# Cross attention in fp32 by three-part products: turned values through a DRAM tile, and an order planned from both ends

## The chip, the cores and the metric

The kernel runs on one core of one Trainium2 chip. The metric is device time in microseconds (us) of one execution of the whole program. TensorE (PE) multiplies, with its weight loads shown apart as PEld; VectorE (DVE), ScalarE (ACT) and GpSimd (POOL) work on elements; SyncE (SP) issues most of the DMA transfers, POOL those that add to their target. Each engine works through its own list of instructions in order. Where an instruction needs another engine's result, it waits at its place in that list, and all that stands behind it on that engine waits as well.

## The reference

There are 32 batches. Of each, `x` and the context `y` have 256 channels and 1024 positions.

```python
x_q = jnp.einsum('oc,bcn->bno', w_qk, y)
x_k = jnp.einsum('oc,bcn->bon', w_qk, x)
x_v = jnp.einsum('oc,bcn->bon', w_v, x) + b_v[None, :, None]
energy = jnp.einsum('bnc,bcm->bnm', x_q, x_k)
attention = jax.nn.softmax(energy, axis=-1)
attention = attention / (1e-07 + attention.sum(axis=1, keepdims=True))
x_r = jnp.einsum('bcn,bnm->bcm', x_v, attention)
x_r = jax.nn.relu(jnp.einsum('oc,bcn->bon', w_t, x - x_r) + b_t[None, :, None])
return x + x_r
```

All of it is in fp32. The shared matrix makes the energies y' (Wqk' Wqk) x, so that one product of weights, made once, serves for queries and keys; likewise w_t goes into the values.

## The kernel before

**Three parts.** A fp32 number is split in three parts in a faster format (`HIGH`, `REST`, `LOW`), and each product is three products of parts that add up in PSUM. So one product of two 256-channel operands to 128 x 1024 results is 12 matmuls of 128x128 by 128x512. PSUM has eight banks of 512 numbers per row, used as four pairs (`pair(0)` to `pair(3)`).

**One batch** is 22 such groups of 12 matmuls, each written as a token: `k0 k1` the keys (`gf` are their three parts), `V0 V1`, or `v0 v1` when made one batch ahead, the values (parts in `uf`), `W0 W1` the straight part w_t x (kept in `xe`), `E0` to `E7` the energies of 128 query positions each (parts of the query side in `yf`), and `A0` to `A7` the attention products, which add up over a whole batch in pairs 2 and 3. Keys, v0 and most energies take pairs 0 and 1 in turn. A token with `^` takes pair 2 or 3 while these are free at a batch's start. The lists `FIRST`, `STEADY`, `BEFORE` and `LAST` set the order of the groups on PE for the first batch, the middle ones, the last but one, and the last.

**Behind an energy group** (`energy`): DVE takes the row minimum (`small`), ACT makes the exponentials in the same banks with their sums, DVE takes the reciprocal, then for each half of 512 columns ACT writes the high part into `ef`, DVE the rest, and DVE adds the scaled half to the column sums `acc`. ACT then makes the low part from the high one, and POOL adds the rest to it. A group has its pair free for the next but one when both engines have read it. An engine that reads a bank waits for another engine that read the same bank earlier in the program.

**Behind a values group** (`values`): DVE turns 32x32 blocks into the tile `turned`; sixteen DMA transfers, issued by SP, carry 32 partitions' pieces from there into `uf`; ACT casts it (`CAST uf`), POOL subtracts, ACT scales, POOL subtracts again. `turned` is one buffer: the next values group's turn waits until the sixteen have landed.

**At a batch's end** (`sums`, `finish`): DVE folds `acc` into reciprocals `rc` and scales pairs 2 and 3 into `z`; POOL adds `xe`, ACT takes the relu, POOL adds `xo` (x once more), SP stores. `load_y` and `load_x` bring the next inputs through `yr` and `xr` and split them, with two POOL-issued adding transfers for `yf` and one per half for `xf`.

**The order.** `Plan` collects every operation with its engine, a cost in us and what it reads and writes. PE's order is that of the tokens. For the other engines and the DMA issues, `order` runs through the program forwards and picks, among the ready operations, the one with the earliest due time. Due times come from a pass back over what depends on each operation. It makes three such orders with different looks ahead and keeps that of the shortest planned span. In the steady batches this gives an order that repeats every two batches.

**Set-up.** Weights and the first x and y are loaded, Wqk' Wqk is made into `gw`, w_t is turned, its product with w_v becomes `vw` (through banks 6 and 7), DVE makes the biases from `wt` and `bv`, and the first keys are made part by part while these appear (tokens `f...` in `SET_UP`).

Of the kernel before, what the change touches and what calls it, by code (L numbers as in the profile page):

```python
# [16 lines left out]
class Plan:  # L17
# [7 lines left out]
    SEEN = 0.1  # L25

# [33 lines left out]
    def order(self):  # L60
        ops = self.ops
        behind, before, last = {}, {}, None
        for op in ops:
            op.feeds = []
        for op in ops:
            for other in op.needs.values():
                other.feeds.append(op)
            if op.engine == "pe":
                if last is not None:
                    behind[last.at], before[op.at] = op, last  # L70
                last = op
        for op in reversed(ops):
            due = [f.due - op.busy - op.lag - self.SEEN for f in op.feeds]
            if op.at in behind:
                due.append(behind[op.at].due - op.busy)
            op.due = min(due, default=0.0) - op.early
        left = [len(op.needs) + (op.at in before) for op in ops]
        can = [0.0] * len(ops)
        free, ready, held, out = {}, {}, 0.0, []
        for op in ops:  # L80
# [3 lines left out]
        while len(out) < len(ops):  # L84
# [6 lines left out]
            t = max(free[engine], can[op.at])  # L91
            busy, done = op.busy, op.busy + op.lag
# [10 lines left out]
            if op.at in behind:  # L103
                nexts.append((behind[op.at], t + busy))
# [8 lines left out]
    def emit(self):  # L113
        best = None
        for look in (0.0, 0.15, 0.3):
            self.LOOK = look
            out = self.order()
            if best is None or self.span < best[0]:
                best = self.span, out
        self.span, out = best  # L120
        for op in out:
            op.trace()

SET_UP = (
    "x0 G fR10 x1 fH11 T fH10 fH01 fH00 Q fL00 fL10 fL11 b y fR00 fR11 fL01 fR01"
)
FIRST = (
    "V0^ W1^ W0^ E0^ E1 E2 V1^ E3 A0 A1 E4 E5 A2 A3 E6 E7 A4 X A5 v0 Y2 k1 A6 A7 k0 Y3 S O"
)
STEADY = (  # L130
    "V1 E0^ E1 W0^ E2 W1^ E3 A0 A1 E4 E5 X A2 A3 E6 E7 A4 S A5 v0 Y2 A6 k1 k0 A7 O Y3"
)
BEFORE = (
    "W1 E0^ E1 V1^ E2 W0^ E3 A0 X A1 E4 A2 E5 Y2 E6 A3 A4 v0 E7 k0 Y3 A5 S A6 k1 A7 O"
)
LAST = (
    "E0 E1^ E2 R V1^ E3 A0 A1 E4 E5 A2 A3 E6 E7 A4 A5 A6 W0 a0 S G0 a1 D1 F1"
# [4 lines left out]
def kernel(  # L142
# [29 lines left out]
    Y_ON_POOL = False  # L172
# [3 lines left out]
    one = ctx.enter_context(tc.tile_pool(name="one", bufs=1))  # L176

# [58 lines left out]
    RC = ["rc"]  # L236
# [15 lines left out]
    turned = one.tile([P, N], F32, name="turned")  # L252
    xe = one.tile([P, KC, N], F32, name="xe")
# [4 lines left out]
    wtb = one.tile([P, KC], F32, name="wtb")  # L258
# [20 lines left out]
    def load_y(q, direct=False):  # L279
# [3 lines left out]
        name = {j: f"yf{s}{j}" for j in ORDER}  # L283
        from_ = y[b].rearrange("(k p) n -> p k n", p=P)[:, :, ts(half, MB)]
        by_sync(7.0 if b else 3.5, ["xr01", "xr11"] if b == 0 else [], ["yr"], lambda: sync.dma_start(r, from_))
        on_act(N, ["yr"], [name[HIGH]], lambda: act.copy(f[:, HIGH], r))
        if direct:
            on_pool(
                N, ["yr", name[HIGH]], [name[REST]],
                lambda: pool.tensor_tensor(f[:, REST], r, value(f[:, HIGH]), ALU.subtract),  # L290
            )
        else:
            on_act(N, [name[HIGH]], [name[REST]], lambda: act.mul(f[:, REST], value(f[:, HIGH]), -1.0))
            by_pool(9.0, [name[REST]], [name[REST]], lambda: accumulate(f[:, REST], from_))
        on_act(N, [name[HIGH]], [name[LOW]], lambda: act.mul(f[:, LOW], value(f[:, HIGH]), 1.0 / UP))
        if direct and q == 0 and Y_ON_POOL:
            on_pool(
                N, [name[LOW], name[REST]], [name[LOW]],
                lambda: pool.tensor_tensor(f[:, LOW], value(f[:, LOW]), value(f[:, REST]), ALU.add),
            )  # L300
        else:
            by_pool(
                8.0, [name[LOW], name[REST]], [name[LOW]],
                lambda: accumulate(value(f[:, LOW]), value(f[:, REST])),
            )
# [65 lines left out]
    def values(b, q, j_pair):  # L371

        both, at, u = pair(j_pair), in_pair(j_pair), uf[q]
        for i in range(KC):
            for j in ORDER:
# [16 lines left out]
        raw = value(u[:, REST])  # L392
        names = [f"uf{q}{j}" for j in range(FORMS)]
        moves = [f"{names[REST]}{a}" for a in range(NG)]
        for a in range(NG):

            def of(a=a):
                for g in range(NG):
                    sync.dma_start(
                        raw[ts(a, G32)].rearrange("p (t g r) -> p t g r", t=HT, g=NG)[:, :, g],  # L400
                        turned[ts(g, G32)].rearrange("p (t a r) -> p t a r", t=HT, a=NG)[:, :, a],
                    )
# [477 lines left out]
```

## Time and profile before

| what | value |
|---|---|
| time, median of 3 runs | 1967.65 us (1963.88 to 1969.02) |
| the profiled execution: its own time | 1967.97 us |
| the profiled execution: its span in the trace | 1966.0 us |
| mean granted TensorE clock | 0.998 |
| busy: PE, DVE, ACT, POOL | 99%, 75%, 74%, 79% of the span |
| DMA | 268.45 MB, 229602 packets, 154976 of them under 512 B |

The span is what the trace shows from the first to the last instruction; the remaining 2 us lie outside it. In rows of the timeline stand start, busy time, engine, line, operation, what is written and read, the count of merged instructions, and in brackets the engine's idle time before it and what ended that. All operations are recorded at one line, that of a helper (L188), so they are told apart by their tiles. Names such as `ef_80` and `uf_74` stand in the program's order for buffers of one name.

### The profile page before, as it was taken

The numbers are of one execution on the slowest core, as the hardware profiler recorded it, in microseconds if no ns is written. First come the engines' busy times: TensorE is split into PE (matmuls) and PEld (weight loads), VectorE is DVE, ScalarE is ACT, GpSimd is POOL, SyncE is SP. The second block draws the span as 40 slices with busy tenths as digits, with TensorE's granted clock in tenths as the row PEclk, the third lists the DMA queues.
The fourth block names the chain that finished last, engine by engine and source line by source line (L and its number), as shares of the span: only waits on it lengthen the run. The fifth ranks groups of instructions, "written<-read, shape, count | busy, mean of one in ns | idle before, by whom it ended". The sixth has DMA issues, their size and how long they took to land.

```text
span 1966.0 us, 25637 instructions
## 1 busy us (share of the span) xinstructions
PE 1939.1 (99%) x8484; PEld 1589.7 (81%) x8484; DVE 1479.4 (75%) x2109; ACT 1448.1 (74%) x1927; POOL 1550.0 (79%) x773
## 2 busy tenths in 40 slices
PE   7999999999999999999999999999999999999998
PEld 6878888888888788888878888888887888888876
DVE  6777777777777777777778777777777777777777
ACT  5687767887677877768867688776687767887675
POOL 4787777888777987778877789777897778888776
PEclk9999999999999999999999999999999999999999
DMA  5655566755566555666556665565665556655552
GB/s 149 127 142 125 138 126 148 171 128 134 127 141 163 134 126 140 129 161 149 120 139 139 144 153 137 131 143 127 152 148 125 136 128 152 165 124 139 106 131 64
DMA packets 229602, 268.45 MB, mean 137 GB/s; under 512 B 154976, under 2 KB 156128, under 8 KB 229472
## 3 DMA queue, kind: packets, MB, share of 16 engines
q1 hardware_dynamic: 193488, 166.81, 29.9%
q0 software_dynamic: 35280, 99.10, 28.7%
q8 instruction: 68, 1.11, 0.2%
q10 hardware_dynamic: 704, 0.92, 0.1%
q14 instruction: 62, 0.51, 0.1%
HBM read 133.56 MB, written 33.55 MB: 85 GB/s over the span
## 4 chain that ended last, share of the span: by engine, by line
ACT 30%; PE 27%; SPq 15%; DVE 13%; issue 6%; DMA 6%; POOL 2%; DVEq 0%; ACTq 0%; POOLq 0%
PE banks L188 27%; SPq L188 15%; ACT ef L188 12%; ACT banks L188 5%; ACT xf L188 4%; DVE ef L188 4%; ACT yf L188 4%; DVE acc L188 3%; ACT uf L188 3%; DVE turned L188 2%; DMA uf<-turned 2%; DMA yr<-in_ctx_dram 2%; DVE small L188 2%; ACT xe L188 2%; POOL uf L188 1%
## 5 line engine op out<-in xcount | busy, mean ns | idle before, releaser
L188 PE MATMUL banks<-gf,yf 128*128 128x512 f32 x3072 | 733.4, 391 | 10.1 <-ACT z L188 3.6
L188 PE MATMUL banks<-ef,uf 128*128 128x512 f32 x3072 | 723.1, 389 | 1.5 <-DVE acc L188 0.9
L188 PEld LDWEIGHTS banks<-gf,yf 128*128 128x128 f32 x3072 | 574.2, 188 | 145.1 <-ACT ef L188 8.6
L188 POOL TENSOR_TENSOR ef<-ef 128x1024 fp32r<-128x1024 f32 x256 | 629.0, 2463 | 72.4 <-ACT ef L188 46.5
L188 PEld LDWEIGHTS banks<-ef,uf 128*128 128x128 f32 x3072 | 576.2, 188 | 122.9 <-POOL ef L188 1.4
L188 DVE SCALAR_TENSOR_TENSOR ef<-banks,small,ef 128x512 fp32r<-128x512 f32 x512 | 381.7, 746 | 177.7 <-ACT ef L188 171.4
L188 POOL TENSOR_TENSOR uf<-uf 128x1024 fp32r<-128x1024 f32 x128 | 326.6, 2551 | 57.2 <-ACT uf L188 57.1
L188 DVE TENSOR_REDUCE small<-banks 128x1 f32<-128x1024 f32 x256 | 310.9, 1215 | 45.1 <-PE banks L188 42.8
L188 ACT ACTIVATE ef<-banks,small 128x512 fp32r<-128x512 f32 x512 | 334.5, 715 | 1.1 <-DVE small L188 1.0
L188 DVE SCALAR_TENSOR_TENSOR acc<-banks,small,acc 128x512 f32<-128x512 f32 x448 | 332.1, 742 | 0.0
L188 ACT ACTIVATE banks<-banks,small 128x1024 f32<-128x1024 f32 x256 | 282.9, 1105 | 64.2 <-DVE small L188 64.2
L188 POOL TENSOR_TENSOR z<-z,xe 128x1024 f32<-128x1024 f32 (+1 forms) x64 | 151.4, 2373 | 205.1 <-DVE z L188 201.2
L188 ACT ACTIVATE ef<-ef 128x1024 fp32r<-128x1024 f32 x256 | 275.9, 1099 | 0.2
L188 ACT ACTIVATE gf<-banks 128x1024 fp32r<-128x1024 f32 x64 | 65.7, 1029 | 216.3 <-PE banks L188 216.3
L188 ACT CAST uf<-uf 128x1024 fp32r<-128x1024 f32 x64 | 68.5, 1070 | 196.4 <-DMA uf<-turned 196.4
L188 PE MATMUL banks<-xf,tw 128*128 128x512 f32 (+1 forms) x774 | 186.4, 390 | 4.9 <-DVE acc L188 4.1
L188 PE MATMUL banks<-xf,vw 128*128 128x512 f32 x768 | 184.6, 389 | 2.9 <-DVE vw L188 2.9
L188 PE MATMUL banks<-xf,gw 128*128 128x512 f32 x768 | 180.6, 390 | 2.8 <-DVE gw L188 2.8
L188 PEld LDWEIGHTS banks<-xf,tw 128*128 128x128 f32 x774 | 145.3, 189 | 36.0 <-ACT ef L188 4.5
L188 PEld LDWEIGHTS banks<-xf,vw 128*128 128x128 f32 x768 | 144.1, 188 | 33.2 <-DVE vw L188 3.3
L188 PEld LDWEIGHTS banks<-xf,gw 128*128 128x128 f32 x768 | 143.9, 188 | 33.4 <-POOL xf L188 3.2
L188 POOL TENSOR_TENSOR z<-z,xo 128x1024 f32<-128x1024 f32 x62 | 156.6, 2526 | 8.8 <-ACT z L188 6.5
(66 smaller groups left out, 1539.2 us busy)
## 6 DMA issues: line engine op xcount, KB each, us to landing
yr<-in_ctx_dram SPq DMA_DIRECT2D x64, 512.0 KB, 3.9
yf<-yf POOLq DMA_DIRECT2D x64, 512.0 KB, 5.3
uf<-turned SPq DMA_DIRECT2D x1024, 32.0 KB, 1.9
yf<-in_ctx_dram POOLq DMA_DIRECT2D x63, 512.0 KB, 6.8
xo<-in_x_dram SPq DMA_DIRECT2D x62, 512.0 KB, 4.4
xr<-in_x_dram SPq DMA_DIRECT2D x62, 512.0 KB, 3.3
xf<-xf POOLq DMA_DIRECT2D x62, 512.0 KB, 6.5
out_dram<-z SPq DMA_DIRECT2D x62, 512.0 KB, 5.0
```

The costliest lines, as they stand in the source:

```text
L188: self.last = getattr(self.engine, name)(*args, **kwargs)
```

## The change

1. **Turned values.** Four transfers write `turned` into a DRAM tile `blocks`, in pieces of 256 numbers instead of 64, and a fifth reads it back with whole rows: into `yr` for the first half of the positions, into `turned` itself for the second. ACT and POOL then split it from there with a four-dimensional pattern. `yr`, which also takes the next y, is thus held until POOL's second subtraction.
2. **Column sums first.** In `halves`, the addition to `acc` stands ahead of the high part. It reads the same bank, so ACT's high part now waits for DVE's addition, where DVE's addition waited for ACT before.
3. **Planner.** A first order is made with the old due times. Then `from_the_end` runs through the program backwards, last to first, with the engines' costs, and gives new due times, which a new forward pass uses; four passes in all, and the shortest planned span is kept. An operation that is not ready yet may be waited for if it is due earlier and PE would be late.
4. **Token lists** are new in all five cases; so is the order within each engine, which repeats every batch now.
5. **Set-up.** w_t and w_v come in halves on two queues, the bias product is four matmuls with one column in place of DVE's multiplication and sum, and the first y is split in two pieces, one on POOL and one by adding transfers.

```diff
 STEADY = (
-    "V1 E0^ E1 W0^ E2 W1^ E3 A0 A1 E4 E5 X A2 A3 E6 E7 A4 S A5 v0 Y2 A6 k1 k0 A7 O Y3"
+    "W0 E0^ E1 E2 V1^ W1^ E3 Y2 X A0 E4 A1 E5 A2 E6 A3 E7 A4 k1 A5 Y3 A6 v0 A7 S k0 O"
 )
...
-                turned.rearrange("p (q i r) -> p i q r", i=KC, r=G32),
-                both.rearrange("p i (q r) -> p i q r", r=G32),
+                turned.rearrange("p (a t i r) -> p i t a r", a=NG, t=HT, i=KC),
+                both.rearrange("p i (t a r) -> p i t a r", t=HT, a=NG),
...
-        for a in range(NG):
-
-            def of(a=a):
-                for g in range(NG):
-                    sync.dma_start(
-                        raw[ts(a, G32)].rearrange("p (t g r) -> p t g r", t=HT, g=NG)[:, :, g],
-                        turned[ts(g, G32)].rearrange("p (t a r) -> p t a r", t=HT, a=NG)[:, :, a],
-                    )
-
-            plan.add("sync", 1.6, 6.0, ["turned"], [moves[a]], of)
-        on_act(N, moves, [names[HIGH]], lambda: act.copy(u[:, HIGH], raw))
+        def out_of():
+            for g in range(NG):
+                sync.dma_start(
+                    blocks.rearrange("(a r) (g s) -> r g a s", a=NG, g=NG)[:, g],
+                    turned[ts(g, G32)].rearrange("p (a s) -> p a s", a=NG),
+                )
+
+        plan.add("sync", 2.4, 2.4, ["turned"], ["blocks"], out_of)
+        back, name = (turned, "turned") if q else (flat(yr), "yr")
+        by_sync(3.2, ["blocks"], [name], lambda: sync.dma_start(back, blocks))
...
+        on_act(N, [name], [names[HIGH]], lambda: act.copy(high, raw))
...
         def halves(h):
             ph, to, a = both[:, h], f[:, :, ts(h, MB)], acc[:, ts(h, MB)]
             high, rest = names[HIGH][h], names[REST][h]
+            if n == 0:
+                on_dve(MB, [at[h], nm[2]], [f"acc{h}"], lambda: dve.tensor_scalar(a, ph, ri, None, ALU.mult))
+            else:
+                on_dve(
+                    MB, [at[h], nm[2], f"acc{h}"], [f"acc{h}"],
+                    lambda: dve.scalar_tensor_tensor(a, ph, ri, a, ALU.mult, ALU.add),
+                )
             on_act(MB, [at[h], nm[2]], [high], lambda: act.mul(to[:, HIGH], ph, ri))
             on_dve(
                 MB, [at[h], nm[2], high], [rest],
...
-            if n == 0:
-                on_dve(MB, [at[h], nm[2]], [f"acc{h}"], lambda: dve.tensor_scalar(a, ph, ri, None, ALU.mult))
...
-            dve.tensor_tensor(product, wt, bv.unsqueeze(1).to_broadcast([P, KC, C]), ALU.mult)
-            dve.tensor_reduce(wtb, product, AX.X, ALU.add)
             dve.tensor_scalar(ubias[:, :, 0], wtb, EPS, None, ALU.mult)
...
+        def product():
+            for i in range(KC):
+                for k in range(KC):
+                    matmul(
+                        wtb[:, i : i + 1], wtT[:, k * C + i * P : k * C + (i + 1) * P], bv[:, k], k == 0, k == KC - 1
+                    )
...
+            op = max((o for o in ready[engine] if can[o.at] <= now), key=lambda o: (o.start, o.at))
+            ready[engine].remove(op)
+            todo -= 1
+            free[engine] = over = now + op.busy
+            op.due = -over - op.early
...
-            within = start + self.LOOK
-            op = min((o for o in ready[engine] if can[o.at] <= within), key=lambda o: (o.due, o.at))
+            op = min((o for o in ready[engine] if can[o.at] <= start), key=lambda o: (o.due, o.at))
+            late = start + op.busy - behind - self.LOOK
+            soon = [o for o in ready[engine] if can[o.at] < start + op.busy and o.due < min(op.due, late)]
+            if soon:
+                op = min(soon, key=lambda o: (o.due, o.at))
```

**The DMA issues of SP.** In a steady batch before, SP's list reads as follows, from one batch's second store (`out_dram`) on. `uf_74` and `uf_75` are the two halves of the values.

```order
L188 DMA out_dram<-z 128x1024
L188 DMA xo<-in_x_dram 128x1024
L188 DMA uf_74<-turned 32x4x64 x16
L188 DMA uf_75<-turned 32x4x64 x16
L188 DMA xo<-in_x_dram 128x1024
L188 DMA out_dram<-z 128x1024
L188 DMA xr<-in_x_dram 128x1024 x2
L188 DMA yr<-in_ctx_dram 128x2x512 x2
```

The same stretch of SP's list in the changed kernel, from the last load of y on:

```order
L231 DMA yr<-in_ctx_dram 128x2x512
L231 DMA blocks<-turned 32x4x256 x4
L231 DMA yr<-blocks 128x1024
L231 DMA xo<-in_x_dram 128x1024
L231 DMA out_dram<-z 128x1024
L231 DMA yr<-in_ctx_dram 128x2x512
L231 DMA out_dram<-z 128x1024
L231 DMA xo<-in_x_dram 128x1024
L231 DMA blocks<-turned 32x4x256 x4
L231 DMA xr<-in_x_dram 128x1024
L231 DMA turned<-blocks 128x1024
L231 DMA xr<-in_x_dram 128x1024
```

Sixteen issues per half have become four and one; one load of y now stands between the two halves, and the read-back of each half waits in SP's list for its four writes.

**ACT at a steady batch's start.** Before, in one of the two batches of the period, ACT's list goes from the keys' high parts (`gf`) to the high parts of E0 (`ef_78`) and E1 (`ef_79`) like this; `banks,small<-banks,small` are the exponentials.

```order
L188 ACTIVATE gf<-banks 128x1024 x2
L188 CAST uf_74<-uf_74 128x1024
L188 ACTIVATE z<-z 128x1024 x2
L188 ACTIVATE banks,small<-banks,small 128x1024
L188 ACTIVATE uf_74<-uf_74 128x1024
L188 ACTIVATE ef_78<-banks,small 128x512
L188 ACTIVATE banks,small<-banks,small 128x1024
L188 ACTIVATE ef_78<-banks,small 128x512
L188 ACTIVATE xe<-banks,xbias 128x1024
L188 ACTIVATE ef_79<-banks,small 128x512 x2
```

In the changed kernel the same stretch, up to the high parts of E2 (`ef_82`; `ef_80` is E0's, `ef_81` E1's). This is the first part of it:

```order
L231 ACTIVATE gf<-banks 128x1024
L231 ACTIVATE z<-z 128x1024
L231 ACTIVATE xe<-banks,xbias 128x1024
L231 ACTIVATE z<-z 128x1024
L231 CAST uf_76<-yr 128x4x4x64
L231 ACTIVATE banks,small<-banks,small 128x1024
L231 ACTIVATE uf_76<-uf_76 128x1024
L231 ACTIVATE banks,small<-banks,small 128x1024
L231 ACTIVATE ef_80<-banks,small 128x512 x2
```

And this is the second, right behind it but for E0's low part and E2's exponentials:

```order
L231 ACTIVATE ef_81<-banks,small 128x512 x2
L231 CAST xf<-xr 128x1024
L231 ACTIVATE xe<-banks,xbias 128x1024
L231 ACTIVATE ef_81<-ef_81 128x1024
L231 CAST xf<-xr 128x1024
L231 ACTIVATE ef_82<-banks,small 128x512 x2
```

The values' cast stands ahead of E0's exponentials in both kernels; the straight part `xe` of W0 has moved ahead of it, and two casts of the next x and the `xe` of W1 stand between the high parts of E1 and E2.

More of the change, by code (lines that the diff above doesn't have):

```diff
@@ L25 @@
     SEEN = 0.1
+    LOOKS = (0.0, 0.3, -0.6, 0.0)
     class Op:
@@ L58, in add, with link @@
         self.ops.append(op)
[L60 to L65, printed above, removed]
+    def link(self):
+        last = None
+        for op in self.ops:
+            op.feeds, op.next, op.before = [], None, None
             for other in op.needs.values():
@@ L102, in order @@
             nexts = [(f, t + done + self.SEEN) for f in op.feeds]
-            if op.at in behind:
-                nexts.append((behind[op.at], t + busy))
+            if op.next is not None:
+                nexts.append((op.next, t + busy))
             for f, when in nexts:
@@ L276, in next_pair, with y_names, load_y @@
         return j
-    def load_y(q, direct=False):
+    NQ = 2
+    QB = MB // NQ
+    def y_names(s, j, pieces=range(NQ)):
+        return [f"yf{s}{j}{q}" for q in pieces]
+    def load_y(q):
         b, half = divmod(q, MH)
@@ L295, in load_y @@
[L295 to L305, printed above, removed]
+        by_sync(7.0 if q else 7.8, [], ["yr"], lambda: sync.dma_start(r, from_))
@@ L307, in x_names @@
+        for which in ([0], [1]) if q == 0 else ([0, 1],):
+            pieces(which)
     def x_names(j, k, halves=range(MH)):
@@ L411, in values @@
         on_pool(
-            N, [names[LOW]], [names[REST]] + moves,
-            lambda: pool.tensor_tensor(u[:, REST], raw, value(u[:, LOW]), ALU.subtract),
+            N, [name, names[LOW]], [names[REST]],
+            lambda: pool.tensor_tensor(rest, raw, value(low), ALU.subtract),
         )
@@ L658, with square @@
     )
-    def square(bank, left, right, reads, writes, blocks=lambda w: w):
+    def square(bank, left, right, reads, writes, blocks_of=lambda w: w):
         for i in range(KC):
@@ L665, in of @@
                     matmul(
[L666 removed]
+                        banks[:, bank + i, :C], left[:, k, ts(i, P)], blocks_of(right[:, k]), k == 0, k == KC - 1
                     )
```

162 lines of the change are left out of this document (99 added, 63 removed).

## The prediction

> **What bounds the kernel now.** I read the page first, then the busy time by stretches, then the timeline where TensorE's share falls, then the waits.
>
> ```profile
> span 1966.0 us, 25637 instructions
> ...
> PE 1939.1 (99%) x8484; PEld 1589.7 (81%) x8484; DVE 1479.4 (75%) x2109; ACT 1448.1 (74%) x1927; POOL 1550.0 (79%) x773
> ```
>
> TensorE is the bound. Its pace is in the timeline of a stretch without an internal wait: two groups of 12 matmuls start 98.49 - 95.77 = 2.72 us apart, so a matmul takes 0.2267 us, and a group's last result comes 0.16 us after the next group could start (2.88 against 2.72).
>
> ```profile
> 95.77 2.88 PE L188 MATMUL banks<-xf,tw 128*128 128x512 f32 x12
> 96.44 1.05 ACT L188 CAST uf<-uf 128x1024 fp32r<-128x1024 f32 x1 [6.39 <-DMA uf<-turned]
> 96.59 1.25 DVE L188 STREAM_TRANSPOSE turned<-banks 128x1024 f32<-128x1024 f32 x1 [5.24 <-DMA uf<-turned]
> ...
> 98.49 2.88 PE L188 MATMUL banks<-gf,yf 128*128 128x512 f32 x12
> ...
> 105.49 1.90 PE L188 MATMUL banks<-xf,tw 128*128 128x512 f32 x6 [4.11 <-DVE acc L188]
> ```
>
> Against that pace I hold the stretches (the first number after the stretch is its length, then PE's busy time and, in brackets, its matmuls):
>
> ```profile
> 0.00:20.00 20.00, 13.22 (x55) 10.39 (x56) 14.45 (x22) 8.81 (x16) 9.77 (x12) 1.00 0.63 199
> 20.00:50.00 30.00, 26.85 (x111) 21.44 (x111) 19.43 (x25) 21.19 (x29) 12.09 (x7) 0.94 0.52 113
> 90.00:112.00 22.00, 17.89 (x73) 14.35 (x72) 11.63 (x16) 13.47 (x19) 14.56 (x8) 0.92 0.40 78
> 112.00:1850.00 1738.00, 1733.18 (x7607) 1424.09 (x7606) 1316.35 (x1872) 1297.19 (x1725) 1393.84 (x691) 1.00 0.61 140
> 1850.00:1966.00 116.00, 107.95 (x469) 86.24 (x467) 86.69 (x132) 78.92 (x107) 86.80 (x41) 0.99 0.37 86
> ```
>
> The first 20 us are set-up. From 20 to 50, 111 matmuls need 25.2 us: 4.8 lost. From 90 to 112, 73 need 16.5: 5.5 lost. From 112 to 1850, 7607 need 1724.5: 13.5 lost, under half a microsecond per batch. From 1850 on, 469 need at most 106.3, so 10 go to waits and the last stores. A change of order can win no more than these sums and a part of set-up. The granted clock (the third number from the right) is 0.94 and 0.92 in the two bad stretches and 1.00 in the steady one: slow matmuls follow the long waits and are part of the loss.
>
> What made the waits? The first one:
>
> ```profile
> 22.82 1.25 DVE L188 STREAM_TRANSPOSE turned<-banks 128x1024 f32<-128x1024 f32 x1 [0.54 <-PE banks L188]
> 24.10 12.63 SPq L188 DMA_DIRECT2D uf<-turned  x15
> ...
> 38.92 1.04 ACT L188 CAST uf<-uf 128x1024 fp32r<-128x1024 f32 x1 [2.18 <-DMA uf<-turned]
> 39.87 1.84 ACT L188 ACTIVATE ef<-banks,small 128x512 fp32r<-128x512 f32 x3
> ...
> 42.14 4.43 PE L188 MATMUL banks<-gf,yf 128*128 128x512 f32 x12 [3.04 <-DVE acc L188]
> ```
>
> The values are turned at 24.07, and ACT can cast them at 38.92: 14.85 us for sixteen small transfers. SP takes 12.63 us for 15 issues, 0.84 each. ACT stands at the cast, the high parts of the energies stand behind it, DVE waits for those, and TensorE waits 3.04 us for a pair. At 96 it is the same: ACT and DVE (whose next turn needs `turned` free) are both released by these transfers, and TensorE stops 4.11 us at 105. In a steady batch the pattern is there, only shorter:
>
> ```profile
> 625.07 1.24 DVE L188 STREAM_TRANSPOSE turned<-banks 128x1024 f32<-128x1024 f32 x1
> ...
> 641.69 1.05 ACT L188 CAST uf<-uf 128x1024 fp32r<-128x1024 f32 x1 [7.50 <-DMA uf<-turned]
> 641.84 1.25 DVE L188 STREAM_TRANSPOSE turned<-banks 128x1024 f32<-128x1024 f32 x1 [2.76 <-DMA uf<-turned]
> ...
> 652.76 2.99 PE L188 MATMUL banks<-gf,yf 128*128 128x512 f32 x12 [0.60 <-ACT z L188]
> ```
>
> Here the way takes 641.69 - 626.31 = 15.4 us, and E3 starts 0.60 us late. Over the run:
>
> ```profile
> ACT uf L188 <- DMA uf<-turned: 196.4, 32, 8.1
> DVE ef L188 <- ACT ef L188: 171.4, 210, 3.5
> ...
> DVE turned L188 <- DMA uf<-turned: 34.3, 15, 5.2
> ```
>
> So TensorE's loss has mostly one origin, the way of the turned values: ACT waited for it 32 times and DVE 15 times.
>
> **The change part by part.** I set TensorE's steady batch as 22 groups of 2.72 us, with zero where W0 starts.
>
> *The way through DRAM.* The trace has no such pair of transfers. Nearest rows (size of one, median us to landing):
>
> ```profile
> xo<-in_x_dram SPq DMA_DIRECT2D x62, 512.0 KB, 4.4
> xr<-in_x_dram SPq DMA_DIRECT2D x62, 512.0 KB, 3.3
> ...
> out_dram<-z SPq DMA_DIRECT2D x62, 512.0 KB, 5.0
> ...
> out_dram<-z SPq DMA_DIRECT2D x2, 128.0 KB, 2.0
> ```
>
> At the low end the four writes of 128 KB land in 2.0 us, all at once, and the read takes 3.3: 5.3 us. At the high end four issues of 0.84, 5.0 for the store and 4.4 for the read make 12.8. I take three issues (2.5), the 128 KB row for the last write (2.0) and the middle of the two reads (3.9), with 0.1 for the hand-over: 8.5 us, since the 128 KB row has the size and the target of these writes. That is 6 us less than 14.85.
>
> When must it be done? v0 ends two groups before the batch does, at -5.44 + 0.16; DVE's turn takes 1.25, so the values are turned at -4.0. ACT has the cast just ahead of E0's exponentials. E0 ends at 5.44 + 0.16, its minimum takes 1.21:
>
> ```profile
> L188 DVE SCALAR_TENSOR_TENSOR ef<-banks,small,ef 128x512 fp32r<-128x512 f32 x512 | 381.7, 746 | 177.7 <-ACT ef L188 171.4
> L188 ACT ACTIVATE ef<-banks,small 128x512 fp32r<-128x512 f32 x512 | 334.5, 715 | 1.1 <-DVE small L188 1.0
> ...
> L188 DVE TENSOR_REDUCE small<-banks 128x1 f32<-128x1024 f32 x256 | 310.9, 1215 | 45.1 <-PE banks L188 42.8
> ...
> L188 ACT ACTIVATE ef<-ef 128x1024 fp32r<-128x1024 f32 x256 | 275.9, 1099 | 0.2
> L188 ACT ACTIVATE xe<-banks,xbias 128x1024 f32<-128x1024 f32 x63 | 71.3, 1132 | 7.7 <-PE banks L188 7.7
> ...
> L188 ACT CAST xf<-xr 128x1024 fp32r<-128x1024 f32 x62 | 66.5, 1074 | 0.0
> ```
>
> The exponentials can start at 6.8 and a cast of 1.05 has to begin by 5.8: the way may take 9.8 us. At 8.5 it is covered by 1.3 us, at 12.8 it is 3 us late, in every batch.
>
> [...]
>
> *The two long waits.* With the way shorter by 6 us, the cast at 38.92 would stand at 33, ahead of the highs that it delayed. The loss from 20 to 50 falls from 4.8 to about 0.4: I count 4.4 (2 to 4.8). From 90 to 112 the same, with `turned` free 6 us earlier and W0 instead of V1 at the front: 5.2 (3 to 5.5), since the 5.24 us of DVE's wait are less than the 6 won. The slow clock behind both waits is inside these sums.
>
> [...]
>
> *Column sums first, and the planned order.* In the rows of a half, ACT's high part (0.715) now comes behind DVE's addition instead of ahead of it. DVE gains: it need not stand idle for the first high part, which is most of its 171.4 us of waiting in 256 groups, 0.67 us each. ACT loses as much latency, and POOL gets its input 0.7 us later, but the attention group comes six groups, 16 us, behind its energy. From E4 on energies and attention now alternate, one energy per 5.44 us where before two stood together; that serves DVE evenly.
>
> The tight place is the start: E0, E1, E2 together, then V1, W1, E3, A0, E4. E4 needs E2's pair at 21.76. W1 ends at 16.48; only then can ACT's list go on: cast, `xe`, E1's low part, cast, E2's first high part, and DVE's rest. With mean durations that is 16.5 + 1.07 + 1.13 + 1.10 + 1.07 + 0.72 + 0.75 = 22.3, late by 0.6. But ACT's rows overlap: three high parts take 1.84, not 2.15, 0.1 less each. So four times 0.1 comes off, and E4 is 0.2 late. I take 0.2 for 29 batches, 6 us (0 to 17, and as much as the 13.5 and 6 more if several such places add up). Of the 13.5 lost there I count 7 as won (-6 to 13).
>
> *Set-up.*
>
> ```profile
> 15.53 1.77 DVE L188 TENSOR_TENSOR xe<-z 128x512 f32<-128x512 f32 x1
> ...
> 17.33 0.69 DVE L188 TENSOR_REDUCE wtb<-xe 128x2 f32<-128x512 f32 x1
> ...
> 19.77 3.01 PE L188 MATMUL banks<-xf,vw 128*128 128x512 f32 x12 [2.90 <-DVE vw L188]
> ```
>
> DVE's 1.77 + 0.69 for the bias product stand ahead of `vw`, for which TensorE waits 2.90. They go to four small matmuls. These wait for `bv`, and `vw`'s product stands behind them on TensorE. I take 2.0 (-1 to 2.9).
>
> *The end.*
>
> ```profile
> 1940.83 2.97 PE L188 MATMUL banks<-gf,yf 128*128 128x512 f32 x12 [1.07 <-ACT ef L188]
> ...
> 1951.52 1.21 PE L188 MATMUL banks<-ef,uf 128*128 128x512 f32 x4 [0.47 <-POOL ef L188]
> ```
>
> W0 now stands ahead of A6, so POOL has 2.72 us more for the wait of 0.47; A3 is set between E5 and E6, which spreads the energies before the wait of 1.07. The other order of the last but one batch puts W1 just two groups behind E0, which may cost that again. I take 2.5 (-2 to 4).
>
> The second half of y's low part, the split weights and the five-dimensional turn I cost at nothing: y's parts are due groups later, and the turn moves as many numbers in runs of 32 as before.
>
> Sum: 4.4 + 5.2 + 7 + 2 + 2.5 = 21.1 us. The profiled execution took 1967.97, 0.3 above the median of 1967.65; against the median, 1946.5.
>
> **The rivals.** *A: the packed start costs more.* If ACT's rows do not overlap behind the new waits for DVE, the 0.6 of the means holds, 29 x 0.4 = 12 us more: 1958.5. For it: ACT now waits for DVE in each half. Against: DVE's own queue is shorter by those 0.67.
>
> *B: the way is late: slower.* Past 9.8 us each microsecond falls on E0's exponentials, W1 and E3, 30 times. To be 6 us slower than before takes 27 us more than I forecast, 0.9 per batch: a way of 10.7 us. At 11.5, 1.7 x 30 = 51 more: 1997. For it: SP's 0.84 per issue and the 5.0 of a store under load. Against: the 2.0 row. [...]
>
> *C: POOL is late instead: no change.* Behind the cast stands POOL's subtraction, ahead of ACT's scaling and E1's exponentials, and in POOL's list three additions for `z` come first. If these are 0.7 us late per batch, 29 x 0.7 = 20 us go: 1966.5. Against: POOL is busy 79%.
>
> **How the numbers follow.** Forecast 0.70, A 0.15, B 0.07, C 0.08. A measurement of this kernel can tell about 0.3%, 6 us, from no change. Faster: forecast, A and a little of C, 0.87. Same: the rest of C, 0.06; slower: B, 0.07. The range: with every gain at its top, 4.8 + 5.5 + 13 + 2.9 + 4 = 30 us, 1937; at the other end it takes in A: 1960. B and C, and the edges, are the two in ten left out.
>
> **What would show it.** Right: ACT's wait for `uf` shrinks from 196.4 to under 60; the way from turn to cast is 7 to 10 us; the clock stays at 1.00 from 20 to 112; the first value matmul starts near 17.8; DVE's wait for `ef` under 60; from 112 to 1850 a loss of some 6, at E4. Wrong: waits of `uf` on the read-back with E0's exponentials behind it (B), of E1's on POOL (C), or a loss in each batch above 0.5 (A).

## The result and the profile after

The changed kernel takes 1946.46 us (median of 4 runs, 1945.59 to 1947.79), the kernel before on the same chip 1965.87 us: a ratio of 0.99, interval 0.9883 to 0.9918. The forecast was 1946.5. That its total fits so well is partly luck: the medians here lie 19.4 us apart where 21.1 were forecast, the kernel before came out 1.8 us below the median that the forecast started from, and errors in the terms cancel, as the point by point section shows. One execution in all the runs (of the way without `yr`, below) went at a granted clock of 0.83 and took 2199.06 us; it is left out there.

The page of the kernel after, its first lines and the chain that ended last:

```profile
span 1943.6 us, 24348 instructions
...
PE 1930.7 (99%) x8492; PEld 1594.9 (82%) x8492; DVE 1496.1 (77%) x2107; ACT 1470.7 (76%) x1929; POOL 1554.5 (80%) x775
...
PE 96%; DMA 1%; DVE 1%; ACT 0%; SPq 0%; POOL 0%; issue 0%; DVEq 0%
```

Every engine is busy for about as long as before; PE is now 96% of the chain itself, where it was 27%. The same stretches as before (the last one ends 22.4 us earlier):

```profile
0.00:20.00 20.00, 17.05 (x67) 13.72 (x68) 10.20 (x20) 9.93 (x19) 10.24 (x14) 0.91 0.73 225
20.00:50.00 30.00, 28.43 (x122) 22.21 (x121) 21.91 (x28) 23.01 (x31) 17.39 (x10) 1.00 0.64 142
90.00:112.00 22.00, 20.56 (x88) 16.11 (x88) 16.13 (x24) 20.02 (x27) 17.79 (x9) 1.00 0.63 190
112.00:1850.00 1738.00, 1738.00 (x7668) 1439.40 (x7668) 1345.05 (x1888) 1333.60 (x1744) 1415.24 (x698) 1.00 0.65 158
1850.00:1943.60 93.60, 86.64 (x377) 70.59 (x375) 72.67 (x107) 58.01 (x78) 61.06 (x31) 0.97 0.38 90
```

I hold them against the same pace of 0.2267 us per matmul. From 112 to 1850 the 7668 matmuls need 1738.3 us, so nothing is lost in 29 batches, where 13.5 us were. From 20 to 50, 2.3 are lost (4.8 before), from 90 to 112 2.05 (5.5), from 1850 on 8.1 (9.7).

The waits that carried the argument (us, times, longest):

```profile
DVE ef L231 <- ACT ef L231: 21.4, 97, 1.4
...
ACT uf L231 <- POOL uf L231: 13.0, 30, 2.5
ACT uf L231 <- DMA yr<-blocks: 11.9, 4, 4.9
```

ACT waits for the read-back of the first half in 4 batches, for 11.9 us; it was 32 times and 196.4. DVE's wait for the first high part fell from 171.4 to 21.4. The way itself, in the timeline of a steady batch:

```profile
620.26 1.25 DVE L231 STREAM_TRANSPOSE turned<-banks 128x1024 f32<-128x1024 f32 x1 [0.50 <-issue]
621.54 2.60 SPq L231 DMA_DIRECT2D blocks<-turned  x4
...
626.38 0.34 SPq L231 DMA_DIRECT2D yr<-blocks  x1
...
630.33 1.03 ACT L231 CAST uf<-yr 128x1024 fp32r<-128x1024 f32 x1
```

From the turn's end (621.51) to the cast is 8.82 us. Four issues take 2.60 and their landing 2.24 more; the read is issued at 626.38, and its landing takes 3.2 us (the median of the DMA view). The remaining 0.75 us ACT spends on `z`: no wait stands in front of the cast. The way takes 8.8 us in nearly every batch, but 11.2 and 12.9 in the first two and 12.8 in the last.

### The profile page after: what moved, and what is told of

Same layout as the page of the kernel before. It is cut to its first block, busy times and chain, and to the rows that moved or that the text cites. A ratio compares the mean times of both kernels' runs of the same rounds, so it can differ in the third digit from the quotient of the medians.

```text
span 1943.6 us, 24348 instructions
## 1 busy us (share of the span) xinstructions
PE 1930.7 (99%) x8492; PEld 1594.9 (82%) x8492; DVE 1496.1 (77%) x2107; ACT 1470.7 (76%) x1929; POOL 1554.5 (80%) x775
## 4 chain that ended last, share of the span: by engine, by line
PE 96%; DMA 1%; DVE 1%; ACT 0%; SPq 0%; POOL 0%; issue 0%; DVEq 0%
PE banks L231 96%; DMA blocks<-turned 1%; DMA yr<-blocks 1%; SPq L231 0%; POOL uf L231 0%; DVE ef L231 0%; DVE z L231 0%; DVE turned L231 0%; DVE acc L231 0%; DVE small L231 0%; POOL z L231 0%; ACT banks L231 0%; ACT uf L231 0%; ACT z L231 0%; ACT xe L231 0%
## 5 line engine op out<-in xcount | busy, mean ns | idle before, releaser
L231 POOL TENSOR_TENSOR ef<-ef 128x1024 fp32r<-128x1024 f32 x256 | 643.3, 2515 | 114.5 <-ACT ef L231 84.4
L231 PE MATMUL banks<-ef,uf 128*128 128x512 f32 x3072 | 731.7, 389 | 0.0
L231 DVE SCALAR_TENSOR_TENSOR ef<-banks,small,ef 128x512 fp32r<-128x512 f32 x512 | 363.2, 741 | 21.6 <-ACT ef L231 21.4
L231 DVE SCALAR_TENSOR_TENSOR acc<-banks,small,acc 128x512 f32<-128x512 f32 x448 | 316.1, 746 | 6.8
L231 POOL TENSOR_TENSOR uf<-yr,uf 128x1024 fp32r<-128x1024 f32 x64 | 153.4, 2397 | 70.3 <-ACT uf L231 70.3
L231 PE MATMUL banks<-xf,gw 128*128 128x512 f32 x768 | 186.5, 392 | 1.9 <-ACT xf L231 1.9
L231 POOL TENSOR_TENSOR uf<-turned,uf 128x1024 fp32r<-128x1024 f32 x64 | 167.6, 2619 | 5.7 <-DVE acc L231 3.3
L231 DVE RECIPROCAL small<-small 128x1 f32<-128x1 f32 x256 | 40.4, 158 | 168.5 <-ACT banks L231 168.5
```

Of the source, the lines that this page charges most:

```text
L231: self.last = getattr(self.engine, name)(*args, **kwargs)
```

## The experiments

Three theories. **Theory 1**: the gain is the shorter way of the turned values, in whatever order. **Theory 2**: it is the new order (lists and planner), and the way is only what that order needs. **Theory 3**: it is DVE, freed from waiting by the column sums. "Steady loss" below is the 1738 us from 112 to 1850 less 0.2267 us for each matmul in it; the row quoted is that stretch. The ratios are those to the kernel before (its median lay between 1968.4 and 1969.3 us in these runs). Differences to the kernel after are differences of medians from different chips; by the ratios they are up to 4 us smaller. In the runs of the first two subsections the planner makes the order anew, so a new order within the engines can come with the edit.

### One part taken out of the kernel after

**Sixteen direct transfers again**, with the old costs in the planner; the rest as after:

```diff
-        plan.add("sync", 2.4, 2.4, ["turned"], ["blocks"], out_of)
-        by_sync(3.2, ["blocks"], [name], lambda: sync.dma_start(back, blocks))
...
+            plan.add("sync", 1.6, 6.0, ["turned"], [moves[a]], of)
```

> The changed kernel with the sixteen direct transfers of before for the turned values; lists, planner, column sums and set-up stay new, and the planner plans with the old cost of the way. Theory 1 (the gain is the shorter way): back to 1960 us or more, ACT's wait for uf over 150 us, and a loss in every steady batch. Theory 2 (the gain is the new order, which hides the way): within 4 us of the changed kernel, 1943 to 1951.

1992.47 us, ratio 1.0115 (1.0099 to 1.0130): 46 us more than after, and slower than before.

```profile
112.00:1850.00 1738.00, 1712.50 (x7468) 1398.28 (x7468) 1309.29 (x1839) 1284.73 (x1701) 1373.45 (x681) 1.00 0.61 138
```

```profile
637.24 11.82 SPq L231 DMA_DIRECT2D uf<-turned  x16
650.61 1.05 ACT L231 CAST uf<-uf 128x1024 fp32r<-128x1024 f32 x1 [2.19 <-DMA uf<-turned]
```

The cast stands 13.4 us behind the first issue, and 45.0 us are lost in steady batches. ACT's wait for `uf` is 63.5 us, not over 150: the planner has put the cast behind E0's exponentials. The new lists without the short way, as the planner then orders them, are worth less than nothing.

**High part first again**, the rest as after:

```diff
...
-                on_dve(
-                    MB, [at[h], nm[2], f"acc{h}"], [f"acc{h}"],
-                    lambda: dve.scalar_tensor_tensor(a, ph, ri, a, ALU.mult, ALU.add),
-                )
             on_act(MB, [at[h], nm[2]], [high], lambda: act.mul(to[:, HIGH], ph, ri))
...
+                on_dve(
+                    MB, [at[h], nm[2], f"acc{h}"], [f"acc{h}"],
+                    lambda: dve.scalar_tensor_tensor(a, ph, ri, a, ALU.mult, ALU.add),
+                )
```

> The changed kernel with the high part ahead of the column sums again. Theory 1 (the way): within 3 us of the changed kernel, 1944 to 1950. Theory 3 (DVE freed from its wait for ACT, 171 us before and 21 after): 8 us or more above it, with E5 and E7 of the steady batches late by 0.1 to 0.3 us each as before, and DVE's wait for ef back over 150 us.

1972.85 us, ratio 1.0022 (1.0013 to 1.0031).

```profile
DVE ef L231 <- ACT ef L231: 142.6, 102, 2.0
```

```profile
112.00:1850.00 1738.00, 1735.53 (x7551) 1412.43 (x7550) 1291.79 (x1862) 1298.64 (x1712) 1388.21 (x688) 1.00 0.63 156
```

DVE's wait is back (142.6 us, a little under the 150 expected), and 26.2 us are lost in steady batches, 0.9 each, with the clock at 1.00. So theory 1 alone is out: the way is even shorter here (7.7 us, median over the 32 first halves), and the time is 26 us longer. How much of that is the edit and how much the new order of ACT's list that came with it (the scaling of `uf` now stands behind E0's high parts) isn't shown. PE's busy time hides the loss (1735.53 of 1738): groups start a little late, at E4, E6 and `k1` and not at E5 and E7, and only the count of matmuls (7551 for 7668) shows it.

**The old planner**, with one pass of due times, on the new lists:

```diff
-        for turn, self.LOOK in enumerate(self.LOOKS):
-            if turn:
-                self.from_the_end()
+        for look in (0.0, 0.15, 0.3):
+            self.LOOK = look
```

> The changed kernel with the old planner: due times by one pass back over the dependences, three looks ahead; lists, way, column sums and set-up stay new. Theory 1 (the way): within 4 us of the changed kernel. Theory 2 in its planner half: 8 us or more above it, by waits at the start of the steady batches, where E2's pair goes to E4.

1948.92 us, ratio 0.9899 (0.9883 to 0.9914), against 0.9883 to 0.9918 for the kernel after. The backward pass can't be told from no effect; the steady stretch loses 2.4 us here.

```profile
112.00:1850.00 1738.00, 1735.48 (x7656) 1437.63 (x7655) 1341.63 (x1884) 1327.96 (x1744) 1410.84 (x698) 1.00 0.64 158
```

### One part put into the kernel before

**The DRAM way alone**, as in after, read back through `yr`:

```diff
+        back, name = (turned, "turned") if q else (flat(yr), "yr")
+        by_sync(3.2, ["blocks"], [name], lambda: sync.dma_start(back, blocks))
```

> The kernel before with nothing but the new way of the turned values: four writes to the DRAM tile and one read. Theory 1 (the way): most of the 20 us, so 1948 to 1954, and the two long waits near 42 and 105 us gone. Theory 2 (the order): 1961 to 1967, since lists and planner are the old ones.

2901.03 us, ratio 1.4731 (1.4710 to 1.4752), which no theory had. SP, POOL and PE in one batch:

```profile
1455.66 0.34 SPq L189 DMA_DIRECT2D yr<-blocks  x1
...
1465.78 2.33 POOL L189 TENSOR_TENSOR uf<-yr,uf 128x1024 fp32r<-128x1024 f32 x1
1468.15 0.40 SPq L189 DMA_DIRECT2D yr<-in_ctx_dram  x1
...
1476.20 2.07 PE L189 MATMUL banks<-gf,yf 128*128 128x512 f32 x4 [12.14 <-ACT yf L189]
...
1495.71 4.47 PE L189 MATMUL banks<-gf,yf 128*128 128x512 f32 x12 [17.44 <-DMA yf<-yf]
```

`yr` has two users now. The old lists load both y halves behind v0, so they wait until POOL has done its second subtraction (1468.11), and PE waits for y: 12.14 and 17.44 us. The new lists have both loads ahead of v0. This tells why the lists had to change with a way through `yr`; it is no test of the way.

**The way without `yr`.** So I read it back straight into `uf`, with four transfers in pieces of 64 numbers (eight transfers in all), and left the lists and the planner as before:

```diff
+                sync.dma_start(
+                    raw[:, ts(t, C)].rearrange("p (g s) -> p g s", g=NG),
+                    blocks.rearrange("p (g t s) -> p t g s", t=HT, g=NG)[:, t],
+                )
+        plan.add("sync", 1.6, 2.8, ["blocks"], [names[REST]], into)
```

> The kernel before, with only its sixteen transfers replaced by the way through the DRAM tile, read back into uf itself by four transfers (eight in all), so that no other buffer is held. Theory 1 (the shorter way is the gain, in whatever order): the two long waits and most of the 13.5 us lost in steady batches go, 1945 to 1955 us, and ACT's wait for uf falls from 196 to under 60 us. Theory 2 (the new order is the gain, the way is only what it needs): 1960 to 1968 us, with TensorE still late at the same groups. Theory 3 (column sums first free DVE): 1958 to 1968 us, with DVE's wait for ef still about 170 us.

2063.16 us (median of three runs, 2056.64 to 2065.28), ratio 1.0467 (1.0444 to 1.0491), again outside every range. ACT's list from the cast on (`banks,small` are E0's exponentials; in the kernel before they stand ahead of the scaling of `uf`, the third row):

```
L189 CAST uf_76<-uf_76 128x1024
L189 ACTIVATE z<-z 128x1024
L189 ACTIVATE uf_76<-uf_76 128x1024
L189 ACTIVATE banks,small<-banks,small 128x1024
```

And a batch of it in the timeline:

```profile
1406.02 1.24 DVE L189 STREAM_TRANSPOSE turned<-banks 128x1024 f32<-128x1024 f32 x1
...
1423.62 1.05 ACT L189 CAST uf<-uf 128x1024 fp32r<-128x1024 f32 x1 [9.18 <-DMA uf<-blocks]
...
1427.17 1.06 ACT L189 ACTIVATE uf<-uf 128x1024 fp32r<-128x1024 f32 x1 [2.50 <-POOL uf L189]
...
1435.06 5.43 PE L189 MATMUL banks<-xf,tw 128*128 128x512 f32 x12 [5.36 <-DVE small L189]
```

Told of a shorter way (9.2 us by its costs instead of 12.4), the planner put the scaling of `uf`, which waits for POOL, ahead of E0's exponentials. The real way took 1423.62 - 1407.26 = 16.4 us here; ACT waited 9.18 for it and 2.50 for POOL, with E0's exponentials behind both, and TensorE stopped for 5.36. So this run changed two things, not one.

**Column sums first alone**, with the edit above in the other direction:

> The kernel before, with only the additions to the column sums put ahead of the high parts. Theory 1: the way of the values is as long as it was, so the two long waits stay and the time is within 4 us of the kernel before. Theory 3: DVE's wait for ef falls to under 60 us and with it the loss in the steady batches, 1945 to 1957 us, although the way is unchanged. Theory 2: within 6 us of the kernel before, either sign.

1977.93 us, ratio 1.0046 (1.0030 to 1.0062): 9 us slower than before. DVE's wait for `ef` falls to 64.4 us from 171.4, and yet the time rises: what an engine waits isn't what TensorE loses by it. Theory 3 as a gain of its own, whatever the lists, is out.

**Both of these**:

> The kernel before, with the way through the DRAM tile (eight transfers, as above) and column sums first, both in the old lists and the old planner. Theory 1 and theory 3 together: 1940 to 1952 us, so that the new lists add nothing of their own. Theory 2: 1958 us or more, since the old lists put two energies together and leave DVE and ACT uneven.

1966.37 us (1958.36 to 1971.22), ratio 0.9982 (0.9968 to 0.9995). The steady stretch is almost what it was:

```profile
112.00:1850.00 1738.00, 1734.20 (x7612) 1425.48 (x7612) 1323.99 (x1874) 1320.63 (x1728) 1396.17 (x692) 1.00 0.65 157
```

12.4 us lost there, against 13.5 before. The two parts together, each slower by itself, come out even in the old lists, each time in the order that the planner made for them.

**Eight transfers in the kernel after**, the same read-back:

> The kernel after, with four transfers for the read-back instead of one, straight into uf: its way is about 1 to 2 us longer than after's 8.8, so 10 to 11 us. If the deadline of 9.8 us that the prediction worked out is sharp, each batch loses 0.2 to 1.2 us: 1952 to 1982 us. If it isn't (theory 1 with slack in the lists), within 4 us of the kernel after: 1945 to 1951 us.

1972.52 us, ratio 1.0015 (1.0005 to 1.0025): 26 us more than after, with a way of 10.2 us (median over the 32 first halves, turn's end to cast) for 8.8.

```profile
112.00:1850.00 1738.00, 1730.15 (x7595) 1422.84 (x7594) 1331.51 (x1872) 1308.67 (x1725) 1397.94 (x691) 1.00 0.66 157
```

16.2 us of it are lost in the steady stretch, most of the rest in the first two batches, where the way takes 14.0 and 16.1 us. The range of the sharp deadline (1952 to 1982) holds it, that of slack (1945 to 1951) doesn't. The planner was told other costs here too, but in the steady batches it kept the order of PE, DVE and POOL and changed ACT's in two places only, both behind E1's exponentials. The way isn't the same in each batch, so the batches show the deadline. The longest of the steady ones:

```profile
816.49 1.25 DVE L231 STREAM_TRANSPOSE turned<-banks 128x1024 f32<-128x1024 f32 x1 [0.45 <-PE banks L231]
...
830.90 1.05 ACT L231 CAST uf<-uf 128x1024 fp32r<-128x1024 f32 x1 [4.18 <-DMA uf<-blocks]
...
838.10 3.01 PE L231 MATMUL banks<-xf,tw 128*128 128x512 f32 x12 [2.62 <-DVE ef L231]
```

The way is 830.90 - 817.74 = 13.16 us, and W1, the last row, starts 2.62 + 0.16 = 2.78 late. In every steady batch with a way above 10.4 us W1 is late by the way less 10.4; E3 behind it is late from 9.9 on; and ways of 9.75 to 9.98 us cost at most 0.2 us.

### The way by itself, every other instruction in its place

The runs above let the planner answer to the edit. In these two it is given the costs of the kernel that they start from, so that PE, DVE, ACT and POOL have that kernel's order, instruction by instruction.

**The kernel before, with the way changed** (eight transfers):

```diff
             def of(a=a):
-                for g in range(NG):
+                if a == 0:
+                    for g in range(NG):
+                        sync.dma_start(
+                            blocks.rearrange("(a r) (g s) -> r g a s", a=NG, g=NG)[:, g],
...
+                elif a == NG - 1:
+                    for t in range(HT):
+                        sync.dma_start(
+                            raw[:, ts(t, C)].rearrange("p (g s) -> p g s", g=NG),
...
             plan.add("sync", 1.6, 6.0, ["turned"], [moves[a]], of)
```

> The kernel before with every instruction of PE, DVE, ACT and POOL in its own order (the planner is given the old costs), only the sixteen transfers of each half replaced by four into the DRAM tile and four back into uf. Theory 1 (the shorter way is the gain): the way falls from 14.4 and 17.4 to 10 or 11 us, the two long waits and most of the 13.5 us of the steady batches go: 1945 to 1955 us. Theory 2 (way and order need each other): the old order was made for a long way, ACT and DVE wait less for uf, but the energies are late all the same: 1958 to 1968 us. If the way under this order's load stays at 14 us, as where the planner reordered it (2064 us), no change: 1963 to 1972 us.

1955.91 us, ratio 0.9941 (0.9922 to 0.9959). The edit alone wins 12.5 us, but not as theory 1 had it:

```profile
90.00:112.00 22.00, 22.00 (x98) 18.22 (x98) 15.60 (x21) 18.84 (x27) 19.42 (x10) 1.00 0.58 141
112.00:1850.00 1738.00, 1735.94 (x7635) 1431.04 (x7634) 1319.36 (x1881) 1303.04 (x1734) 1403.07 (x695) 1.00 0.66 157
```

```profile
ACT uf L189 <- DMA uf<-blocks: 190.1, 32, 8.0
```

ACT still waits 190.1 us for `uf`, because the way of the first half is hardly shorter: 13.8 us (median) for 14.4, of which the writes take 8.5 until the read can be issued. That is the case of the expectation in which nothing should have changed, 1963 us or more; it missed what the buffer is worth. DVE's wait for `turned` (34.3 us, 15 times, before) is gone: the writes into the DRAM tile have left that buffer 8.5 us after the first half's turn (median, to the issue of the read), where sixteen transfers held it for 14.2. The second long wait is gone with it (98 matmuls need 22.2 us), and the steady loss is 7.1 for 13.5; the first long wait stays (4.04 us at 42.72). What is shown of theory 1 here is the buffer; the latency in the old order is not tested, since it stayed.

**The kernel after, with one more transfer in the way**, from `blocks` to a second DRAM tile:

```diff
-        by_sync(3.2, ["blocks"], [name], lambda: sync.dma_start(back, blocks))
+        def hopped():
+            sync.dma_start(hop, blocks)
+            sync.dma_start(back, hop)
+
+        by_sync(3.2, ["blocks"], [name], hopped)
```

> The kernel after with every instruction in its place, and one more transfer in the way, from the DRAM tile to a second one: estimated 3.2 to 4.9 us by the rows of the read-backs, so a way of 12 to 14 us. If the deadline of 9.8 us is sharp, as rival B had it (each microsecond past it falls on every batch): 2.2 to 4.2 us in 30 batches, 2010 to 2070 us. If the lists have slack behind it, as the run with sixteen transfers has it (1.4 us per batch at a way of 14 us or more): 1960 to 1985 us.

2141.46 us, ratio 1.0884 (1.0861 to 1.0907): the sharp deadline, and worse. One steady batch and the stretch:

```profile
623.35 1.21 DVE L231 STREAM_TRANSPOSE turned<-banks 128x1024 f32<-128x1024 f32 x1
...
634.06 0.34 SPq L231 DMA_DIRECT2D yr<-hop  x1
...
638.42 1.05 ACT L231 CAST uf<-yr 128x1024 fp32r<-128x1024 f32 x1 [5.31 <-DMA yr<-hop]
...
645.55 4.54 PE L231 MATMUL banks<-xf,tw 128*128 128x512 f32 x12 [3.66 <-DVE ef L231]
```

```profile
112.00:1850.00 1738.00, 1639.42 (x6975) 1337.55 (x6974) 1218.88 (x1721) 1212.82 (x1592) 1286.54 (x636) 0.97 0.63 161
```

The way is 638.42 - 624.56 = 13.86 us, 4.06 past the deadline of 9.8. W1, the last of these rows, starts 3.66 + 0.16 = 3.82 late, and its matmuls take 4.54 for 2.88. Over the steady batches the way goes from 11.9 to 15.1 us, and in each of them W1 is late by the way less 10.0 to 10.4. The stretch holds 6975 / 264 = 26.4 batches and loses 156.8 us, 5.9 in each: 3.3 are W1's lateness, 1.8 its slow matmuls and what follows at E3, and 0.8 stand at E6 and A3, for a reason that isn't looked into here. So the deadline, and the price of one for one behind it, hold, with nothing else moved on these four engines; the slow matmuls behind W1's wait come on top (the granted clock of the stretch is 0.97, where after has 1.00). With sixteen transfers the way is as long (13.4), yet a batch loses 45.0 / 28.3 = 1.6: there the planner knew of it and put the cast behind E0's exponentials, in after it stands ahead of them.

### A version that is faster

The one long wait left in after behind set-up is at E3 of the last batch:

```profile
1871.59 1.25 DVE L231 STREAM_TRANSPOSE turned<-banks 128x1024 f32<-128x1024 f32 x1
...
1885.68 1.05 ACT L231 CAST uf<-yr 128x1024 fp32r<-128x1024 f32 x1 [4.91 <-DMA yr<-blocks]
1886.83 2.38 POOL L231 TENSOR_TENSOR uf<-yr,uf 128x1024 fp32r<-128x1024 f32 x1 [10.52 <-ACT uf L231]
...
1889.24 1.06 ACT L231 ACTIVATE uf<-uf 128x1024 fp32r<-128x1024 f32 x1 [2.51 <-POOL uf L231]
...
1895.94 4.61 PE L231 MATMUL banks<-gf,yf 128*128 128x512 f32 x12 [2.63 <-DVE ef L231]
```

The way takes 1885.68 - 1872.84 = 12.8 us here. POOL has been idle for 10.52 us when the cast is done; ACT's scaling waits for POOL's subtraction, and E0's exponentials stand behind both. So v0 goes one group forward in the last batch but one:

```diff
 BEFORE = (
-    "V1 E0^ E1 W0^ W1^ E2 A0 E3 E4 A1 A2 Y2 E5 E6 A3 E7 S A4 X Y3 A5 v0 A6 k1 k0 A7 O"
+    "V1 E0^ E1 W0^ W1^ E2 A0 E3 E4 A1 A2 Y2 E5 E6 A3 E7 S A4 X Y3 v0 A5 A6 k1 k0 A7 O"
```

> The kernel after, with v0 one group earlier in the last but one batch (ahead of A5). The one long wait behind set-up, 2.63 us at 1896 with 1.4 us of slow clock, comes from ACT's and POOL's splitting of these values ahead of the last batch's first exponentials; 2.7 us earlier they are out of the way: 4 us less, 1941 to 1944 us. If the wait is set by the energies that stand together there (E0, E1 and E2, E3 with one group between), it stays: 1945 to 1948 us.

1942.18 us (1941.38 to 1942.65), ratio 0.9871 (0.9853 to 0.9888). The interval touches that of the kernel after, but all four times lie below its four, the span is 3.8 us shorter, and the wait is gone:

```profile
1850.00:1939.80 89.80, 85.29 (x377) 69.17 (x375) 72.06 (x107) 58.20 (x78) 60.95 (x29) 1.00 0.38 92
```

The same 377 matmuls take 89.8 us for 93.6, at a clock of 1.00 for 0.97. ACT's wait for POOL is as long as before (2.52 us) but ends at 1885.65 instead of 1889.24: what was late was the way, and not POOL.

## Why the prediction was right, point by point

**The way: right in the steady batches.** Forecast 8.5 us, measured 8.82: issues 2.60 (2.5), write 2.24 (2.0), read 3.2 (3.9), and 0.75 in which ACT was still at other work. Behind the last issue the two legs took 2.24 + 3.2 = 5.4; the low end of the rows had made 2.0 + 3.3 = 5.3.

**The deadline of 9.8 us: right.** Measured by the two longer ways it is 9.9 (E3) to 10.4 us (W1), with one for one behind it. Rival B is therefore a real mechanism; its condition, a way past the deadline, held in the first two batches and the last, and in none of the others. Its price left out the slow matmuls behind such a wait (4.54 us for 2.88 in the longer of these ways).

**The two long waits: right in kind, mis-sized.** Forecast 4.4 and 5.2, measured 4.8 - 2.3 = 2.5 and 5.5 - 2.05 = 3.4. The step that failed is taking the steady way for the first two batches:

```profile
21.98 1.25 DVE L231 STREAM_TRANSPOSE turned<-banks 128x1024 f32<-128x1024 f32 x1 [0.31 <-PE banks L231]
23.26 3.29 SPq L231 DMA_DIRECT2D blocks<-turned  x4
...
34.40 1.05 ACT L231 CAST uf<-yr 128x1024 fp32r<-128x1024 f32 x1 [1.84 <-DMA yr<-blocks]
...
40.45 1.90 PE L231 MATMUL banks<-gf,yf 128*128 128x512 f32 x7 [1.45 <-DVE ef L231]
```

Here it takes 34.40 - 23.23 = 11.2 us, past the deadline, and E3 is late by 1.45. In the second batch it takes 12.9.

**The steady stretch: mis-sized, 13.5 won instead of 7.** The failed step is E4's 0.2 us. I set the cast behind W1's end in the chain. In the trace it starts ahead of it (W1's last result is there at 641.93):

```profile
639.05 2.88 PE L231 MATMUL banks<-xf,tw 128*128 128x512 f32 x12
...
641.07 1.04 ACT L231 CAST xf<-xr 128x1024 fp32r<-128x1024 f32 x1
...
642.01 1.12 ACT L231 ACTIVATE xe<-banks,xbias 128x1024 f32<-128x1024 f32 x1
...
644.90 1.27 ACT L231 ACTIVATE ef<-banks,small 128x512 fp32r<-128x512 f32 x2
...
645.83 1.40 DVE L231 SCALAR_TENSOR_TENSOR ef<-banks,small,ef 128x512 fp32r<-128x512 f32 x2
...
647.21 2.88 PE L231 MATMUL banks<-gf,yf 128*128 128x512 f32 x12
```

DVE's first half (0.7 of its 1.40) is done at 646.5, ahead of E4, which starts on time. Rival A falls with the same rows.

**Column sums first: the effect seen, its weight not.** The forecast had DVE's wait at under 60 us (21.4), but gave it no price of its own. In the new lists it is worth 26 us, in the old ones it costs 9, each time with the order that the planner made for it. ACT's high parts now wait for DVE's additions to `acc`, 33 times and 9.7 us in all.

**Set-up: mis-sized.** Forecast 2.0; the first value matmul starts at 18.92 instead of 19.77, 0.85. DVE's 2.46 us are gone and TensorE's wait for `vw` with them, but the first stretch's clock is 0.91 where it was 1.00:

```profile
8.53 3.15 PE L231 MATMUL banks<-xf,gw 128*128 128x512 f32 x8 [1.89 <-ACT xf L231]
```

Eight matmuls take 3.15 us behind a wait of 1.89, at a granted clock of 0.63 (8.53 to 11.68); at the pace they need 1.97. Those 1.2 us would account for what is missing.

**The end: mis-sized.** 1.6 for 2.5. The risk that the forecast named, the new order of the last batches, came true at another place: E3 of the last batch, behind a way of 12.8 us (rival B's mechanism, once). Rival C did not come: ACT waits for POOL's subtraction 30 times, 13.0 us in all, and no steady batch loses by it.

Measured, the terms are 0.85 + 2.5 + 3.4 + 13.5 + 1.6 = 21.9 of the 22.4 us by which the profiled time fell. Four terms measured 5.7 us less than forecast, one 6.5 more: that these cancel is luck.

**The cause.** The forecast's reason, TensorE's loss has mostly one origin, holds for the kernel after: with every other instruction in its place a longer way falls on W1 one for one, and the long waits left in it stand where the way is still long. As an attribution of the gain it is too simple. Taken out of after, the way costs 46 us and column sums first 26, both with an order that the planner made anew; put into before, column sums first cost 9, and the way with the order kept gives 12.5, though by the buffer, since the way itself stayed at 13.8 us. They are not terms that add. Theory 1 holds for the kernel after and for the buffer, theory 2 for the need of lists that fit, theory 3 only within the new lists, where it is mixed with a new order; none holds alone. How the gain divides among the lists, the way, the column sums and set-up stays open: no run has a way below the deadline in the old order, and none takes the column sums out of after with after's order kept.

## What to carry to other kernels

A step with a deadline costs nothing while it meets it and, here, one microsecond for each past it: work out the deadline from the engine's list, and test it with an added delay while all else stays in place. Where a planner sets the order, a changed cost or dependence is a second edit; keep the order to test the first one alone. When a buffer gets a second user, look at every load that is queued behind it: this one cost 930 us in the old lists.

## What the runs showed of the hardware

Slow matmuls followed some waits of TensorE and not others (12 matmuls take 2.88 us at the pace). In before, 3.04 us of waiting at 42.14 and 4.11 at 105.49 were followed by 12 matmuls in 4.43 and 4.46 us, with a granted clock of 0.65 and 0.63 over these. In after, 12 matmuls took 4.61 behind 2.63 us at 1895.94 (0.63), and 8 took 3.15 behind 1.89 us at 8.53 (0.63 too); in the run with the added transfer 12 took 4.54 behind the 3.66 us at 645.55. It isn't the length alone: behind the 2.90 us at 19.77 in before (in set-up) 12 took 3.01 at a clock of 1.00, and in the run with eight transfers in the kernel after, 12 took 3.01 behind the 2.62 us at 838.10 (1.00 from 838.0 to 841.5). What else it takes is not shown.

SP's issues are not of one price: in after, four writes of 128 KB to DRAM took 2.60 us to issue at 621 and 3.29 at 23.
